# Inner Winograd sums in another order, and one subtraction and one right sum moved ahead, in a cross-attention kernel

## The chip, the cores and the metric

The kernel runs on one core of a Trainium2 chip. The metric is the device time in microseconds of one execution; three executions of the kernel before took 667.75, 667.77 and 668.99 us, a median of 667.77 us. The profile is of one further execution, which took 667.35 us, of which 665.4 us are the span from its first to its last instruction. All times of single instructions below are microseconds from the start of that span.

A core has five engines that run their own instruction streams in order and wait for one another through semaphores. Short names in the profile: PE is TensorE (matmul; PEld its weight loads), DVE is VectorE, ACT is ScalarE, POOL is GpSimd, SP is SyncE, which only issues DMAs here. GpSimd issues DMAs too, those that accumulate into on-chip memory among them.

## The reference

Eight batches of cross attention, all in fp32. `C1 = C2 = 512` channels, `N = 1024` positions, `D = 64`:

```python
q = jnp.einsum('bcn,dc->bnd', x1, Wq) + bq
k = jnp.einsum('bcn,dc->bdn', x2, Wk) + bk[:, None]
v = jnp.einsum('bcn,dc->bdn', x2, Wv) + bv[:, None]
attn = jax.nn.softmax(jnp.einsum('bnd,bdm->bnm', q, k), axis=2)
attn_out = jnp.einsum('bcm,bnm->bcn', v, attn)
return attn_out + x1
```

## The kernel before, in words

**Order of the mathematics.** The value projection is pulled behind the softmax. For each batch the kernel computes the scores transposed (`e`, two halves of 512 query positions each, 1024 keys in four tiles of 128 for each of two key groups), subtracts the column maximum (`top`), takes the exponential, then `y = x2 * e` (512 x 1024 by 1024 x 1024), scales `y` by the reciprocal of the column sums (`den`), and then `o = Wv * y`, to which `bv` and `x1` are added.

**Winograd products.** Both matrix products (stage "y" and stage "o") are split into quadrants 11, 12, 21, 22 and done with Winograd's seven products in place of eight. Left quadrants are `a` (of x2, transposed) or `w` (of Wv), right quadrants `t` (of `e`) or `y`. Sums S1 to S4 are made of the left quadrants, T1 to T4 of the right ones. The table `MULT` names the seven products by number: 1 is 11 x 11, 2 is 12 x 21, 6 is S2 x T2, 7 is S3 x T3, 5 is S1 x T1, 3 is S4 x 22, 4 is 22 x T4. Several of the seven are split once more in the same way; these have inner sums, which VectorE makes just before: `left_stream` (line 550) writes the tile `aI` of four 128x256 pieces from `LEFT` or `LEFT_SUM`, and `right_stream` (lines 573, 578, 583, 585) writes `eI`. For products 1 and 2 the four right sums are four separate instructions (line 573), since their sum is also used for the column sums (`total_0`, line 282); for the others T1 and T3 are one instruction (line 578), then T2 (583), then T4 (585). For batch n these tiles are called `aI1`, `eI2` and so on by the product; `o1`, `o7` and `o3` are products of stage "o".

**Inner products on TensorE.** `multiply_seeded` (stage "y") runs the seven inner products of one product in the order 1, 7, 6, 2, 5, 4, 3: it builds a running sum in a PSUM bank (`chain`), and ScalarE copies (line 787) seed the result's four parts from it between the steps. The step of inner product 6 goes on accumulating into `chain` only when ScalarE has copied it out. The seeds of product 1 go into bank a, those of product 2 into bank c.

**What sets the order around the change.** The schedule is written by hand: each engine's instructions run in the order in which the Python code emits them, and `weave` alternates between streams, one instruction of each in turn. `period` emits one batch `s` together with the next batch `n`: products of `y` for `s`, scores of `n`, then stage "o" of `s` while the maximum of `n` is taken off its scores (`lower`, line 340) and exponentials run on ScalarE (`exponential`, line 349), and at last the first sums of `n`. For the periods of batches 1 to 6 (`five`; `six` is batches 2 to 5), the end of the period goes like this:

- `multiply_41` interleaves product 4 of stage "y" with product 1 of stage "o". Between them `highest` folds the maximum of half 1 (line 266), and GpSimd's all-reduce (line 272) spreads it over the partitions. `complete` (line 874) closes each bank on VectorE; `evict_y` (930) and `scale_y` (916) give quadrant 21 of y, which the product of `second(2)` reads (line 485, `ps_oc<-y,w`).
- the remaining subtractions of the maximum (340) are woven with the right sums of product 7 of stage "o" (578, 583, 585, tile `eIo7`, tag `eT1`).
- `left_stream(n, 1, ...)` makes the left sums of the next batch's product 1, woven with a subtraction.
- `multiply_57` runs products 5, 7 and 3 of stage "o"; ScalarE's last seed of it is line 752. On VectorE, `complete` (line 760) waits for that seed, and `evict_o(s, "22")` (line 978, `uo`) reads quadrant 22 out; after it TensorE adds product 4 onto the same banks (`second(4)`, line 485, `ps_oc<-yT,w`).
- `early_s2` on ScalarE (`negate`, line 177) and GpSimd (an accumulating DMA, line 181) starts S2 of the next batch.
- `sum_e` (358) makes T1 of the next batch from all four tiles of `e`, `sum_t3` (384) accumulates T3 by two DMAs, then the woven right and left sums of products 1 and 2 follow, `total_0`, and `evict_o(s, "21")` (978, `o<-ps_oc`), which frees bank c.

Of the kernel before, what the change touches and what calls it, by code (L numbers as in the profile page):

```python
# [15 lines left out]
def kernel(  # L16
# [483 lines left out]
    def multiply_o1(s):  # L500
# [9 lines left out]

    LEFT = (
        ("S3", "11", "21", ALU.subtract),
        ("S1", "21", "22", ALU.add),
        ("S2", "11", "S1", ALU.subtract),
        ("S4", "12", "S2", ALU.add),
    )
    def weave(*streams):
# [13 lines left out]
    def in_turn(*streams):  # L531
# [3 lines left out]

    LEFT_SUM = (
        ("S3", "21", "11", ALU.subtract),
        ("S1", "21", "22", ALU.subtract),
        ("S2", "11", "S1", ALU.subtract),
        ("S4", "12", "S2", ALU.subtract),  # L540
    )

# [13 lines left out]
    def right_stream(s, i, x, *tags):  # L556

        half = x.shape[1] // 2
        v = {f"{q + 1}{r + 1}": x[:, ts(q, half), ts(r, H // 2)] for q in range(2) for r in range(2)}
        last = 4 // len(tags)  # L560
        shape = [P, last, half, H // 2]
        sums = [sb.tile(shape, F32, tag=t, name=f"eI{i}{t}_{s.b}") for t in tags]
        if i in (1, 2):
            for z, k in enumerate(("T1", "T2", "T4", "T3")):
                v[k] = sums[z // last][:, z % last]
            s.inner[i, "t"], s.inner[i, "m"] = v, sums[-1][:, last - 2 : last]
            for k, x, y, op in (
                ("T1", "12", "11", ALU.subtract),
                ("T3", "22", "12", ALU.add),
                ("T2", "T1", "22", ALU.add),  # L570
                ("T4", "21", "T2", ALU.subtract),
            ):
                nc.vector.tensor_tensor(v[k], v[x], v[y], op)
                yield
            return
        both, t2, t4 = sums[0][:, 0:2], sums[-1][:, last - 2], sums[-1][:, last - 1]
        part = x.rearrange("p (q k) (r n) -> p q k r n", q=2, r=2)
        nc.vector.tensor_tensor(
            both, part[:, :, :, 1, :], part[:, 0].rearrange("p k r n -> p r k n"), ALU.subtract
        )  # L580
        s.inner[i, "t"] = v | {"T1": both[:, 0], "T3": both[:, 1], "T2": t2, "T4": t4}
        yield
        nc.vector.tensor_tensor(t2, both[:, 0], v["22"], ALU.subtract)
        yield
        nc.vector.tensor_tensor(t4, v["21"], t2, ALU.add)
        yield
# [567 lines left out]
    def period(s, n, nn, nnn):  # L1154
# [54 lines left out]
        def early_s2():  # L1209
            negate(n, "S2")  # L1210
            add_11(n, "S2")
# [225 lines left out]
        if five:  # L1437
            fold(n, 1, 3, "max", ALU.max)
            products = multiply_41(s)
            next(products)  # L1440
            highest(n, 1)
            next(products, None)
            if nn:
                copy_yt4(s)
# [21 lines left out]
        if five:  # L1466
            if nn is None:
                scale_y(s, "22")
            sum_y(s, "T1")
            weave(  # L1470
                in_turn(lowers(n, 0, 2 + s.six, MH), lowers(n, 1, 0, 2)),
                right_stream(s, "o7", s.y["T3"], "eT1"),
            )
        if s.b == 0:
            add_tile(n, 0, 1)
# [32 lines left out]
        if n:  # L1508
            if five:
                sums_1 = left_stream(n, 1, n.a["11"], "i2")  # L1510
                next(sums_1)
                weave(
                    sums_1, singly(lambda: lower(n, 1, 2), *([] if nn else [lambda: sum_y(s, "T4")]))
                )
        if n is None:
            inner_right(s, "o3", s.y["22"], "eT2")
# [1 line left out]
        elif late:  # L1518
            complete_7 = multiply_57(s, while_57)
            if five:  # L1520
                if nn is None:
                    exponential(n, 1, 1)
                exponential(n, 1, 2)
                early_s2()
        else:
            complete_7 = multiply_57(s, lambda j: early_s2() if j else None)
# [10 lines left out]
            complete_7()  # L1537
        if n:
            leave = evict_o(s, "22")
        if five:  # L1540
            exponentials(n, 1, 3)
        if five:
            open_t(n)
            if nn:
# [73 lines left out]
```

## Time and profile before

| what | us |
|---|---|
| median of the runs shown (3) | 667.77 |
| profiled execution | 667.35 |
| its span | 665.4 |
| TensorE busy | 659.8 (99%) |
| VectorE busy | 626.3 (94%) |
| ScalarE busy | 379.1 (57%) |
| GpSimd busy | 208.8 (31%) |
| VectorE waiting ahead of line 760, five times | 6.2 |
| VectorE waiting ahead of line 874 of product 4, five times | 4.9 |

The granted clock is 1.0 throughout. How to read what follows: a row of the timeline gives the start, the time from the first start to the last end of the merged records, the engine, line, operation, written tile and read tiles, sizes, and how many records were merged; in brackets stands the idle time of the engine just before and what released it. Every fp32 matmul of the program is two records. Matmuls are pipelined and the ends of their records are modelled: a matmul that waits reads as busy, so stalls are found from the distances between starts. On the other engines a record's duration is some 0.08 us longer than its pitch, the distance at which the next independent instruction follows.

### The profile page before, as it was taken

The numbers are of one execution on the slowest core, as the hardware profiler recorded it, in microseconds if no ns is written. First come the engines' busy times: TensorE is split into PE (matmuls) and PEld (weight loads), VectorE is DVE, ScalarE is ACT, GpSimd is POOL, SyncE is SP. The second block draws the span as 40 slices with busy tenths as digits, with TensorE's granted clock in tenths as the row PEclk, the third lists the DMA queues.
The fourth block names the chain that finished last, engine by engine and source line by source line (L and its number), as shares of the span: only waits on it lengthen the run. The fifth ranks groups of instructions, "written<-read, shape, count | busy, mean of one in ns | idle before, by whom it ended". The sixth has DMA issues, their size and how long they took to land.

```text
span 665.4 us, 7983 instructions
## 1 busy us (share of the span) xinstructions
PE 659.8 (99%) x2626; PEld 432.7 (65%) x2626; DVE 626.3 (94%) x890; ACT 379.1 (57%) x727; POOL 208.8 (31%) x179
## 2 busy tenths in 40 slices
PE   9999999999999999999999999999999999999997
PEld 4435755766667666677666686576865757666865
DVE  1999999999999999999999999899998999999997
ACT  3755556456574575665766646756567556474332
POOL 0126215641235403263033530345213540224300
PEclk9999999999999999999999999999999999999999
DMA  9698578993889759897598895987928994376614
GB/s 334 251 287 269 107 252 154 201 284 108 276 174 216 180 155 285 180 220 197 149 280 181 197 237 162 250 175 178 272 58 189 212 211 179 74 155 160 119 40 150
DMA packets 47368, 129.05 MB, mean 194 GB/s; under 512 B 5472, under 2 KB 5984, under 8 KB 47328
## 3 DMA queue, kind: packets, MB, share of 16 engines
q0 software_dynamic: 20336, 55.12, 45.9%
q1 hardware_dynamic: 26848, 73.29, 29.7%
q8 instruction: 21, 0.34, 0.2%
q14 instruction: 19, 0.16, 0.1%
q10 hardware_dynamic: 144, 0.14, 0.1%
HBM read 87.83 MB, written 16.81 MB: 157 GB/s over the span
## 4 chain that ended last, share of the span: by engine, by line
PE 87%; DVE 11%; issue 1%; ACT 0%; DVEq 0%; ACTq 0%
PE ps_yc L596 8%; PE ps_ya L596 6%; PE ps_s L236 6%; PE ps_oa L730 6%; PE ps_oc L485 6%; PE ps_q L191 4%; PE ps_oa L485 4%; PE ps_k L191 3%; PE ps_ya L485 3%; PE ps_i7chain L596 3%; PE ps_i5chain L596 3%; PE ps_i4b L881 3%; PE ps_i3chain L596 3%; PE ps_i2chain L596 2%; PE ps_oc L881 2%; PE ps_i4chain L881 2%
## 5 line engine op out<-in xcount | busy, mean ns | idle before, releaser
L349 ACT ACTIVATE e<-e 128x1024 f32<-128x1024 f32 x60 | 63.4, 1058 | 24.4 <-DVE e L340 23.9
L340 DVE TENSOR_TENSOR e<-e,top 128x1024 f32<-128x1024 f32 x60 | 72.2, 1216 | 0.2 <-POOL top L272 0.2
L272 POOL PARTITION_ALL_REDUCE top<-max x16 | 32.0, 2000 | 104.7 <-DVE max L266 62.9
L245 ACT COPY e<-ps_s 128x512 f32<-128x512 f32 x90 | 47.7, 619 | 10.2 <-PE ps_s L236 10.1
L304 POOL PARTITION_ALL_REDUCE den<-sum x10 | 33.4, 3336 | 44.1 <-DVE sum L266 39.2
L236 PE MATMUL ps_s<-q,k 64*128 64x512 f32 (+1 forms) x188 | 46.6, 598 | 0.0
L256 DVE TENSOR_TENSOR max<-max,e 128x1024 f32<-128x1024 f32 x30 | 36.5, 1217 | 0.3
L236 PEld LDWEIGHTS ps_s<-q,k 64*128 64x128 f32 x188 | 17.5, 186 | 19.9 <-issue 17.3
L916 DVE TENSOR_TENSOR y<-y,den 128x1024 f32<-128x1024 f32 x24 | 29.2, 1219 | 0.3
L550 DVE TENSOR_TENSOR aI<-a,aI 128x256 f32<-128x256 f32 x60 | 28.1, 468 | 1.1
L787 ACT COPY ps_yc<-ps_i7chain 128x256 f32<-128x256 f32 x32 | 11.4, 357 | 30.3 <-PE ps_i7chain L596 25.6
L730 PE MATMUL ps_oa<-yT,w_S 128*128 128x512 f32 x56 | 27.5, 592 | 0.0
L285 POOL PARTITION_ALL_REDUCE den<-sum x6 | 19.4, 3228 | 25.1 <-DVE sum L266 25.1
L730 PE MATMUL ps_oa<-y,w_S 128*128 128x512 f32 x56 | 26.3, 592 | 0.0
L191 PE MATMUL ps_q<-x_in_x_dram,wqk_sb 128*64 128x512 f32 x112 | 25.6, 598 | 0.0
L787 ACT COPY ps_ya<-ps_i5chain 128x256 f32<-128x256 f32 x32 | 11.5, 360 | 24.1 <-PE ps_i5chain L596 20.0
L485 PE MATMUL ps_oa<-yT,w_S 128*128 128x512 f32 x56 | 25.2, 593 | 0.0
L485 PE MATMUL ps_oc<-yT,w 128*128 128x512 f32 x56 | 25.2, 592 | 0.0
L550 DVE TENSOR_TENSOR aI<-a 128x256 f32<-128x256 f32 x60 | 24.0, 425 | 0.0
L596 PE MATMUL ps_yc<-e,aI 128*128 128x256 f32 x92 | 23.6, 379 | 0.0
L325 POOL DMA_DIRECT2D den<-row x12 | 6.7, 560 | 53.1 <-DMA row<-few 42.3
L983 POOL DMA_DIRECT2D r<-in_x_dram x14 | 18.3, 1309 | 15.5 <-ACT r L971 15.5
(354 smaller groups left out, 1838.7 us busy)
## 6 DMA issues: line engine op xcount, KB each, us to landing
x_in_x_dram<-in_x_dram SPq DMA_DIRECT2D x60, 512.0 KB, 7.2
a<-in_x2T_dram SPq DMA_DIRECT2D x32, 512.0 KB, 5.8
aS<-in_x2T_dram POOLq DMA_DIRECT2D x21, 512.0 KB, 7.0
eT<-eT POOLq DMA_DIRECT2D x16, 512.0 KB, 11.8
r<-in_x_dram POOLq DMA_DIRECT2D x14, 512.0 KB, 7.1
uo<-in_x_dram POOLq DMA_DIRECT2D x14, 512.0 KB, 8.2
out_dram<-r SPq DMA_DIRECT2D x14, 512.0 KB, 3.3
e<-e POOLq DMA_DIRECT2D x13, 512.0 KB, 6.7
```

The source lines that it names most:

```text
L191: nc.tensor.matmul(ps[r, :], w_sb[:, c, :], s.x[:, c, ts(h, H)], start=(c == 0), stop=(c == CT - 1),)
L236: nc.tensor.matmul(ps[g][:, n], s.k[r, ts(i, P)], s.q[r, ts(h, H)][:, n], start=True, stop=True)
L245: nc.scalar.copy(e[:, g, i, :], ps[g])
L256: nc.vector.tensor_tensor(f, e[:, :, 0, :] if i == 1 else f, e[:, :, i, :], op)
L304: nc.gpsimd.partition_all_reduce(s.den[h], s.mx[h][:, 0, :], P, ReduceOp.add)
L340: nc.vector.tensor_tensor(e, e, top, ALU.subtract)
L349: nc.scalar.activation(e, e, AF.Exp)
L485: nc.tensor.matmul(ps, left[ka][:, k, ts(j, P)], right[kb][:, k, :], start=opens and k == 0, stop=i in (2, 3, 4) and k == n_k - 1, skip_gr ...
L550: nc.vector.tensor_tensor(v[k], v[x], v[y], op)
L596: nc.tensor.matmul(ps, s.inner[i][ka][:, k, :], s.inner[i, "t"][kb][:, k, :], start=opens and k == 0, stop=z in (2, 3, 4) and k == n_k - 1 ...
L730: nc.tensor.matmul(ps, w[ka][:, k, ts(j, P)], s.y[kb][:, k, :], start=False, stop=i == 3 and k == 1, skip_group_check=True,)
L881: nc.tensor.matmul(ps, s.inner[i][ka][:, k, :], s.inner[i, "t"][kb][:, k, :], start=opens and k == 0, stop=z in (2, 3, 4) and k == n_k - 1 ...
```

## The change

Three kinds of edits, all of order; no tile, shape or count of instructions changes.

1. **Inner sums.** The left sums of `LEFT` and `LEFT_SUM` go from S3, S1, S2, S4 to S3, S2, S1, S4. S2 is made from S3 and quadrant 22 instead of quadrant 11 and S1, which is the same sum. The separate right sums of products 1 and 2 go from T1, T3, T2, T4 to T3, T2, T1, T4, with T2 made from T3 and quadrant 11.
2. **Last subtraction of the maximum.** For batches 1 to 6, `lower(n, 1, 3)` and `exponential(n, 1, 3)` stood together behind `evict_o(s, "22")`. The subtraction is now woven into the left sums of the next product 1, ahead of `multiply_57`'s `complete`, and the exponential stands ahead of `early_s2`.
3. **A right sum of product 7 of stage "o".** The first instruction of `right_stream(s, "o7", ...)` (T1 and T3 at once, line 578) is emitted inside `multiply_41`, behind `highest` and ahead of the second `complete`; the rest of the stream stays where it was.

```diff
     LEFT = (
         ("S3", "11", "21", ALU.subtract),
+        ("S2", "S3", "22", ALU.subtract),
         ("S1", "21", "22", ALU.add),
-        ("S2", "11", "S1", ALU.subtract),
         ("S4", "12", "S2", ALU.add),
     )
...
     LEFT_SUM = (
         ("S3", "21", "11", ALU.subtract),
+        ("S2", "22", "S3", ALU.subtract),
         ("S1", "21", "22", ALU.subtract),
-        ("S2", "11", "S1", ALU.subtract),
         ("S4", "12", "S2", ALU.subtract),
     )
...
             for k, x, y, op in (
+                ("T3", "22", "12", ALU.add),
+                ("T2", "T3", "11", ALU.subtract),
                 ("T1", "12", "11", ALU.subtract),
-                ("T3", "22", "12", ALU.add),
-                ("T2", "T1", "22", ALU.add),
                 ("T4", "21", "T2", ALU.subtract),
             ):
...
             products = multiply_41(s)
             next(products)
             highest(n, 1)
+            sums_o7 = right_stream(s, "o7", s.y["T3"], "eT1")
+            next(sums_o7)
             next(products, None)
...
                 in_turn(lowers(n, 0, 2 + s.six, MH), lowers(n, 1, 0, 2)),
-                right_stream(s, "o7", s.y["T3"], "eT1"),
+                sums_o7,
             )
...
                 weave(
-                    sums_1, singly(lambda: lower(n, 1, 2), *([] if nn else [lambda: sum_y(s, "T4")]))
+                    sums_1,
+                    singly(lambda: lower(n, 1, 2), *([] if nn else [lambda: sum_y(s, "T4")]), lambda: lower(n, 1, 3)),
                 )
...
                 exponential(n, 1, 2)
+                exponential(n, 1, 3)
                 early_s2()
...
             leave = evict_o(s, "22")
-        if five:
-            exponentials(n, 1, 3)
         if five:
             open_t(n)
```

The order of instructions at three places on VectorE, each in the period of batch 3, whose next batch is 4 (in a tile's name the batch follows the name: `y21_3`, `aI1_4`). First the end of products 4 and o1; before:

```order
L874 TENSOR_TENSOR ps_oc1_3_1_2229<-ps_oc1_3_1_2229,v41_3_2232 128x512
L266 TENSOR_TENSOR max_4_1_2214<-max_4_1_2214 128x512
L874 TENSOR_TENSOR ps_i4b1_3_2227<-ps_i4b1_3_2227,v41_3_2232 128x512
L930 TENSOR_TENSOR y21_3_2279<-uy6_3_2027,ps_i4b1_3_2227 128x512
L930 TENSOR_TENSOR y21_3_2279<-uy6_3_2027,ps_i4b0_3_2226 128x512
L916 TENSOR_TENSOR y21_3_2279<-y21_3_2279,den_3_0_1853 128x1024
L447 TENSOR_TENSOR yT1_3_2217<-y22_3_2152,yT2_3_2218 128x1024
L340 TENSOR_TENSOR e_4_0_1987<-e_4_0_1987,top_4_0_2043 128x2x512
L578 TENSOR_TENSOR eIo7eT1_3_2286<-yT3_3_2160 128x512
```

and with the change:

```order
L874 TENSOR_TENSOR ps_oc1_3_1_2229<-ps_oc1_3_1_2229,v41_3_2232 128x512
L266 TENSOR_TENSOR max_4_1_2214<-max_4_1_2214 128x512
L578 TENSOR_TENSOR eIo7eT1_3_2265<-yT3_3_2160 128x512
L874 TENSOR_TENSOR ps_i4b1_3_2227<-ps_i4b1_3_2227,v41_3_2232 128x512
L930 TENSOR_TENSOR y21_3_2281<-uy6_3_2027,ps_i4b1_3_2227 128x512
L930 TENSOR_TENSOR y21_3_2281<-uy6_3_2027,ps_i4b0_3_2226 128x512
L916 TENSOR_TENSOR y21_3_2281<-y21_3_2281,den_3_0_1853 128x1024
L447 TENSOR_TENSOR yT1_3_2217<-y22_3_2152,yT2_3_2218 128x1024
```

Line 578 of product o7 moved up past six instructions, to stand between the fold of the maximum and the second line 874. Second the left sums of the next product 1 up to T1 of the next batch; before:

```order
L550 TENSOR_TENSOR aI1_4_2310<-a11_4_2163 128x256 x2
L340 TENSOR_TENSOR e_4_1_2165<-e_4_1_2165,top_4_1_2263 128x2x512
L550 TENSOR_TENSOR aI1_4_2310<-a11_4_2163,aI1_4_2310 128x256 x2
L573 TENSOR_TENSOR eI1yT2_4_2350<-e_4_0_1987 128x512
L760 TENSOR_TENSOR ps_oc1_3_7_2317<-ps_oc1_3_7_2317,vo7_3_2320 128x512
L978 SCALAR_TENSOR_TENSOR uo5_3_2321<-ps_oc0_3_7_2316,wqk_sb_69,uo5_3_2321 128x512
L978 SCALAR_TENSOR_TENSOR uo5_3_2321<-ps_oc1_3_7_2317,wqk_sb_69,uo5_3_2321 128x512
L340 TENSOR_TENSOR e_4_1_2165<-e_4_1_2165,top_4_1_2263 128x2x512
L358 TENSOR_TENSOR eT1_4_2358<-e_4_1_2165,e_4_0_1987 128x1024 x2
```

and with the change:

```order
L550 TENSOR_TENSOR aI1_4_2310<-a11_4_2163 128x256
L550 TENSOR_TENSOR aI1_4_2310<-a11_4_2163,aI1_4_2310 128x256
L340 TENSOR_TENSOR e_4_1_2165<-e_4_1_2165,top_4_1_2263 128x2x512
L550 TENSOR_TENSOR aI1_4_2310<-a11_4_2163 128x256
L340 TENSOR_TENSOR e_4_1_2165<-e_4_1_2165,top_4_1_2263 128x2x512
L550 TENSOR_TENSOR aI1_4_2310<-a11_4_2163,aI1_4_2310 128x256
L573 TENSOR_TENSOR eI1yT1_4_2353<-e_4_0_1987 128x512
L760 TENSOR_TENSOR ps_oc1_3_7_2318<-ps_oc1_3_7_2318,vo7_3_2321 128x512
L978 SCALAR_TENSOR_TENSOR uo5_3_2322<-ps_oc0_3_7_2317,wqk_sb_69,uo5_3_2322 128x512
L978 SCALAR_TENSOR_TENSOR uo5_3_2322<-ps_oc1_3_7_2318,wqk_sb_69,uo5_3_2322 128x512
L358 TENSOR_TENSOR eT1_4_2358<-e_4_1_2165,e_4_0_1987 128x1024 x2
```

The second line 340 moved up past the last left sum, the first right sum, line 760 and both lines 978; the left sums changed their order, and the first right sum (573) writes the buffer `yT1` instead of `yT2`. Third the sums of product 6 of batch 4; before:

```order
L550 TENSOR_TENSOR aI6_4_2431<-aS2_4_2347 128x256
L578 TENSOR_TENSOR eI6yT2_4_2433<-eT2_4_2359 128x1024
L550 TENSOR_TENSOR aI6_4_2431<-aS2_4_2347 128x256
L583 TENSOR_TENSOR eI6y21_4_2434<-eI6yT2_4_2433,eT2_4_2359 128x512
L550 TENSOR_TENSOR aI6_4_2431<-aS2_4_2347,aI6_4_2431 128x256
L585 TENSOR_TENSOR eI6y21_4_2434<-eT2_4_2359,eI6y21_4_2434 128x512
```

and with the change:

```order
L550 TENSOR_TENSOR aI6_4_2431<-aS2_4_2349 128x256
L578 TENSOR_TENSOR eI6yT2_4_2433<-eT2_4_2359 128x1024
L550 TENSOR_TENSOR aI6_4_2431<-aI6_4_2431,aS2_4_2349 128x256
L583 TENSOR_TENSOR eI6y21_4_2434<-eI6yT2_4_2433,eT2_4_2359 128x512
L550 TENSOR_TENSOR aI6_4_2431<-aS2_4_2349 128x256
L585 TENSOR_TENSOR eI6y21_4_2434<-eT2_4_2359,eI6y21_4_2434 128x512
```

The second left sum is now S2, which reads S3 of its own tile, and the third is S1. On ScalarE the exponential of the last tile (line 349) moved from behind the negation of line 177 to ahead of it. The orders of TensorE, GpSimd and SyncE are unchanged.

## The prediction, made before the changed kernel ran

> **What bounds the kernel now.** I read busy time by stretches first, then TensorE's own instructions in order of time, then what VectorE and ScalarE did at each place where TensorE's pitch breaks.
>
> ```profile
> 200.00:281.70 81.70, 81.18 (x331) 55.26 (x330) 78.32 (x113) 49.48 (x96) 27.71 (x24) 1.00 0.82 203
> 281.68:362.47 80.79, 80.79 (x330) 54.94 (x329) 77.43 (x112) 49.56 (x96) 27.66 (x24) 1.00 0.83 206
> ...
> 443.26:524.05 80.79, 80.79 (x329) 54.93 (x329) 77.45 (x112) 49.56 (x96) 27.69 (x24) 1.00 0.77 179
> ```
> The columns are the stretch, its length, then busy time on TensorE, its weight loads, VectorE, ScalarE and GpSimd, the granted clock, DMA share and GB/s. The middle periods (batches 3, 4 and 5; the first and last are shown) are equal to 10 ns, TensorE is busy in all of each, and VectorE has 3.3 us to spare. So TensorE's instruction stream sets the pace. But a stalled matmul still reads as busy here, since ends are modelled, so the starts must be read. This is TensorE around the start of batch 4:
>
> ```profile
> 364.04 1.03 PE L596 MATMUL ps_i2chain<-e,a 128*128 128x256 f32 x4
> 364.90 1.03 PE L596 MATMUL ps_i2third<-eI2eT,aI 128*128 128x256 f32 x4
> 365.89 1.13 PE L596 MATMUL ps_i2chain<-eI2eT,aI 128*128 128x256 f32 x4
> 366.86 1.03 PE L596 MATMUL ps_yc<-e,a 128*128 128x256 f32 x4
> ...
> 371.18 1.03 PE L596 MATMUL ps_i6third<-eI6yT,aI 128*128 128x256 f32 x4
> 372.17 1.10 PE L596 MATMUL ps_i6chain<-eI6y,aI 128*128 128x256 f32 x4
> 373.11 1.03 PE L596 MATMUL ps_ya<-eT,aS 128*128 128x256 f32 x4
> ```
> A group of four records has a pitch of 0.86 us (364.04 to 364.90). The third inner product of product 2 starts 0.13 late (0.99 after its forerunner), and its own group then takes 0.97, 0.11 more. Product 6 shows the same: 0.99 and 0.94. That is 0.24 and 0.21 us of stall in each period, and both are the inner product 6 of MULT, the one that reads S2 and T2. The start of batch 2 (first pair) is worse, that of batch 6 (second pair) like batch 4:
>
> ```profile
> 202.76 1.03 PE L596 MATMUL ps_i2third<-eI2eT,aI 128*128 128x256 f32 x4
> 204.31 1.13 PE L596 MATMUL ps_i2chain<-eI2eT,aI 128*128 128x256 f32 x4 [0.52 <-ACT ps_yc L787]
> ...
> 526.48 1.03 PE L596 MATMUL ps_i2third<-eI2eT,aI 128*128 128x256 f32 x4
> 527.48 1.13 PE L596 MATMUL ps_i2chain<-eI2eT,aI 128*128 128x256 f32 x4
> ```
> In batch 2 the gap is 1.55, 0.69 too long, and with 0.10 of restart 0.79 is lost; in batch 6 it is 1.00, so 0.24 with the restart. What is late:
>
> ```profile
> 364.65 1.40 DVE L978 SCALAR_TENSOR_TENSOR o<-ps_oc,wqk_sb,uo 128x512 f32<-128x512 f32 x2
> ```
> ```profile
> 365.48 0.36 ACT L787 COPY ps_yc<-ps_i2chain 128x256 f32<-128x256 f32 x1 [0.78 <-DVE o L978]
> ```
> ```profile
> 371.62 0.41 DVE L550 TENSOR_TENSOR aI<-aS,aI 128x256 f32<-128x256 f32 x1
> ```
> Product 2 of the new batch takes the bank that still holds the old batch's result quadrant 21. VectorE reads that out at 364.65, only then ScalarE seeds the bank (365.48 to 365.84), and TensorE goes on at 365.89. For product 6, the S2 sum ends at 372.03 and TensorE starts at 372.17. Both stalls are VectorE being late after the period's turn, not VectorE being short of time.
>
> **The change part by part.** It adds and removes no arithmetic: every sum, subtraction, exponential and DMA keeps its shape. Only order moves, so the prices are of waits.
>
> *The right sum of product 7, moved ahead.* VectorE waits before line 874, which closes the bank of product 4, and the moved sum fits there:
>
> ```profile
> 337.64 0.70 DVE L874 TENSOR_TENSOR ps_i4b<-ps_i4b,v 128x512 f32<-128x512 f32 x1 [0.99 <-ACT ps_i4b L890]
> ...
> 339.70 1.22 DVE L916 TENSOR_TENSOR y<-y,den 128x1024 f32<-128x1024 f32 x1
> ```
> ```profile
> 341.24 3.60 PE L485 MATMUL ps_oc<-y,w 128*128 128x512 f32 x8
> ```
> The wait of 0.99 starts at 336.65; the sum (0.6 us of pitch, 128x512, in SBUF) ends by 337.3, so line 874 starts where it did, and 0.6 us is saved later. If it did not fit, line 916, which ends at 340.92 for the products of 341.24, has 0.3 us before TensorE waits. Price between 0 and, if the whole sum were added, 0.3 a period; I take 0, since 0.6 is less than 0.99.
>
> *The last subtraction of the maximum, moved ahead.* Line 340 for the last tile of half 1 stood behind line 760, where VectorE also waits:
>
> ```profile
> 346.65 0.75 DVE L550 TENSOR_TENSOR aI<-a 128x256 f32<-128x256 f32 x2
> ...
> 348.46 0.87 DVE L550 TENSOR_TENSOR aI<-a,aI 128x256 f32<-128x256 f32 x2
> ...
> 351.28 0.70 DVE L760 TENSOR_TENSOR ps_oc<-ps_oc,vo 128x512 f32<-128x512 f32 x1 [1.35 <-ACT ps_oc L752]
> ...
> 353.51 1.22 DVE L340 TENSOR_TENSOR e<-e,top 128x1024 f32<-128x1024 f32 x1
> 354.64 2.43 DVE L358 TENSOR_TENSOR eT<-e,e 128x1024 f32<-128x1024 f32 x2
> ```
> Today the left sums end at 349.3. Less 0.6 for the sum moved above, plus 1.13 for the subtraction (its pitch, 353.51 to 354.64), they end near 349.8. Then comes the first right sum of the next product 1. It is T3 now, and in batches 3 to 5 it is written over the old T1 of y, which TensorE still reads:
>
> ```profile
> 348.97 1.02 PE L730 MATMUL ps_oa<-yT,w_S 128*128 128x512 f32 x2
> ```
> Those reads end at 349.99, so T3 runs from about 350.0 to 350.6, still ahead of the 351.28 at which line 760 is released by ScalarE. The new wait costs nothing while it ends 0.6 before the old one; without that cover it would cost what it runs over. So line 760 does not move, and all behind line 978 moves up by the 1.13 of the subtraction. Behind it line 978's read-out of quadrant 21 comes at 363.5 instead of 364.65. The bank is then free before TensorE's first inner product ends (364.90), ScalarE copies at once, and the stall of 0.24 is gone. In batch 2 the same 1.13 exceeds the 0.69. Product 6's sums come 1.13 earlier too, and its stall of 0.21 goes.
>
> *ScalarE.* The exponential that belongs to the moved subtraction goes ahead of the negation that starts S2 of the next batch:
>
> ```profile
> 352.12 1.05 ACT L177 ACTIVATE aS<-aS 128x1024 f32<-128x1024 f32 x1
> 354.76 1.06 ACT L349 ACTIVATE e<-e 128x1024 f32<-128x1024 f32 x1 [1.59 <-DVE e L340]
> ...
> 363.64 1.06 ACT L156 ACTIVATE aS<-aS 128x1024 f32<-128x1024 f32 x1
> ```
> ```profile
> aS<-in_x2T_dram POOLq DMA_DIRECT2D x21, 512.0 KB, 7.0
> ```
> The exponential runs in the 1.59 of wait, so the two sums of line 358 don't wait for it. The negation, and on GpSimd's queue the accumulating DMA of S2, come 1.0 later: issued about 354.5, landed near 361.5 by the median of 7.0. The reader is line 156 at 363.64, ScalarE's next step ahead of the seeds, so 2 us are left. On that queue the two accumulations of T3 stand behind S2's DMA; they wait for line 358, which is earlier by more than the 1.0. I take 0; bounds 0 to 0.5 a period if a DMA lands late.
>
> *Order of the inner sums.* Two unrelated 128x256 sums take 0.75, two dependent ones 0.87. Unwoven, S3, S1, S2, S4 has two dependent neighbours, S3, S2, S1, S4 one: 0.12 us of VectorE per group saved, where nothing waits for it. For product 6, S2 now stands before the T2 sum instead of behind it, 0.3 earlier: it would cure that stall alone, so it isn't counted twice. T1, T3, T2, T4 and T3, T2, T1, T4 have one dependent pair each: no difference.
>
> *Sum of the middle.* Three periods lose 0.24 + 0.21, batch 2 loses 0.79 + 0.21, batch 6 loses 0.24: 1.35 + 1.00 + 0.24 = 2.59 us, all taken as gained.
>
> **The last two batches.** From batch 6 VectorE has no wait to fill (no wait is noted at these rows), so moved work delays what it passes:
>
> ```profile
> 576.21 2.36 DVE L916 TENSOR_TENSOR y<-y,den 128x1024 f32<-128x1024 f32 x2
> ...
> 589.78 1.40 DVE L978 SCALAR_TENSOR_TENSOR uo<-ps_oc,wqk_sb,uo 128x512 f32<-128x512 f32 x2
> ```
> ```profile
> 577.72 3.60 PE L485 MATMUL ps_oc<-y,w 128*128 128x512 f32 x8
> ...
> 591.04 3.60 PE L485 MATMUL ps_oc<-yT,w 128*128 128x512 f32 x8
> ...
> 619.48 1.03 PE L596 MATMUL ps_i7chain<-e,a 128*128 128x256 f32 x4
> 620.97 1.13 PE L596 MATMUL ps_i7third<-eI7yT,aI 128*128 128x256 f32 x4 [0.47 <-DVE eI7yT L578]
> 622.00 1.10 PE L596 MATMUL ps_i7chain<-eI7yT,aI 128*128 128x256 f32 x4
> ```
> The scaling for the products of 577.72 ends at 577.4 (half of line 916's row); with 0.6 ahead of it, 578.0: TensorE loses 0.4 and 0.1 of restart. Line 978's first half ends at 590.5 for the products of 591.04; with 1.13 + 0.12 ahead it ends at 591.8, when TensorE would be at 591.5: 0.3 + 0.1 more. That is 0.9. But TensorE waits later for VectorE anyhow: 619.48 to 622.00 is 2.52 where two groups take 1.73, a stall of 0.79. VectorE's total of work up to there is the same, so the 0.9 comes out of that stall, and about 0.1 is left; the dependent pairs give back as much. I take 0 for the tail, bounds -0.3 to +0.9.
>
> Against the profiled execution's own 667.35 (span 665.4 and 1.95 around it) the sum is 667.35 - 2.59 = 664.8. The median of the runs shown is 667.77, 0.42 higher; from it the forecast is 667.77 - 2.59 = 665.2 us.
>
> **The rivals.** *The tail pays.* VectorE ends later as well, so the stall at 620.97 stays and the 0.9 comes on top: 665.2 + 0.9 = 666.1. For it: VectorE is back to back there, and any new wait adds in full. Against: the same instructions in the same stretch.
>
> *The stalls stay.* ScalarE's copy or another condition ends right behind VectorE's, or the T3 sum misses its slot: 667.8. For it: at 365.89 the wait is on ScalarE by its own line. Against: that copy notes VectorE as its releaser, with 0.78 of waiting.
>
> *The moved sum is held by GpSimd's all-reduce*, which starts in the very gap it is moved to. This one ends slower:
>
> ```profile
> 336.83 1.78 POOL L272 PARTITION_ALL_REDUCE top<-max  x1 [8.09 <-DVE max L266]
> ```
> ```profile
> 147.14 1.78 POOL L272 PARTITION_ALL_REDUCE top<-max  x1 [3.49 <-DVE max L266]
> ```
> ```profile
> 147.55 1.70 DVE L578 TENSOR_TENSOR eI3eT<-e 128x1024 f32<-128x1024 f32 x1
> ```
> At 147.55 a line 578 that started inside such an all-reduce took 1.70 and ended 0.33 after it; the first row of line 916 above gives 1.22 for that size. Held likewise, the moved sum would end at 338.9, line 874 and the scaling would come 1.25 later, and the scaling would end at 342.2 for products at 341.24: 0.9 + 0.1 lost in each of five periods. 665.2 + 5.0 = 670.2. It decides as soon as the hold passes 0.3 us. Against it: the sum starts about 336.65, 0.2 before the all-reduce. The Trainium skill (SBUF — State Buffer, Who interferes with whom) says that a VectorE instruction with two SBUF inputs and a GpSimd instruction that reads SBUF share a port, and that whichever starts first keeps it for the whole instruction. The row at 147.55 agrees; by that rule the order of two starts 0.2 us apart decides between 665.2 and 670.2.
>
> **How the numbers follow.** Forecast 0.62, tail 0.13, stalls stay 0.13, held sum 0.12. A difference of 0.2% (1.3 us) is about what a measurement here can tell from none. Faster by more than that are the forecast but for a twentieth, and most of the tail's case: 0.70; within it the stays and the rest: 0.18; slower the held sum: 0.12. The likeliest alone spans 664.4 (the tail's stall gone too, 0.79) to 666.1. The range reaches up to 667.8 to take in the tail and most of the stays, and leaves out the held sum.
>
> **What would show it.** Right: the gap before line 760 under 0.7 us; line 874's wait down by 0.6 with its start unmoved against TensorE; quadrant 21 read out 1.1 us earlier against product 2; a pitch of 0.86 through products 2 and 6; middle periods of 80.35 us; new waits of 0.3 to 0.5 in batch 6 and a smaller one before product 7 of batch 7. Wrong: a line 578 of over 1 us beside the all-reduce, a wait at line 485 in the middle periods, line 156 waiting for its DMA, or periods still 80.79.

## The result and the profile after

The changed kernel takes 665.51 us (median of 8 runs, 664.88 to 666.81), the kernel before, run beside it, 668.09 us (median of 8, 667.51 to 669.51). The ratio is 0.9961 with a 95% interval of 0.995 to 0.9972: 2.6 us less. The profiled execution of the changed kernel took 665.49 us, with a span of 663.5.

Busy time by stretches first, as before: the first and the last of the three middle periods (batches 3 and 5), from one place of a batch to the same place of the next, with the same columns.

```profile
281.35:361.70 80.35, 80.35 (x330) 55.10 (x329) 77.31 (x112) 49.56 (x96) 27.69 (x24) 1.00 0.84 206
...
442.04:522.39 80.35, 80.35 (x330) 55.11 (x329) 77.30 (x112) 49.55 (x96) 27.71 (x24) 1.00 0.77 180
```

A period is 80.35 us where it was 80.79, and VectorE's work in it is 0.12 to 0.15 less (77.31 where it was 77.43, 77.30 where it was 77.45). TensorE still reads as busy throughout, so the gain is invisible in the busy share. It stands in the starts. TensorE at product 2 and product 6 of batch 4:

```profile
363.26 1.03 PE L596 MATMUL ps_i2chain<-e,a 128*128 128x256 f32 x4
364.12 1.03 PE L596 MATMUL ps_i2third<-eI2eT,aI 128*128 128x256 f32 x4
364.99 1.03 PE L596 MATMUL ps_i2chain<-eI2eT,aI 128*128 128x256 f32 x4
365.85 1.03 PE L596 MATMUL ps_yc<-e,a 128*128 128x256 f32 x4
...
370.17 1.03 PE L596 MATMUL ps_i6third<-eI6yT,aI 128*128 128x256 f32 x4
371.03 1.03 PE L596 MATMUL ps_i6chain<-eI6y,aI 128*128 128x256 f32 x4
371.89 1.03 PE L596 MATMUL ps_ya<-eT,aS 128*128 128x256 f32 x4
```

Every group stands 0.86 or 0.87 behind its forerunner. The 0.99 and 0.97 of product 2, and the 0.99 and 0.94 of product 6, are gone. In batch 2, where 0.79 was lost, the same:

```profile
203.43 1.03 PE L596 MATMUL ps_i2third<-eI2eT,aI 128*128 128x256 f32 x4
204.30 1.03 PE L596 MATMUL ps_i2chain<-eI2eT,aI 128*128 128x256 f32 x4
```

VectorE shows why. Its rows from the end of the products 4 and o1 to the read-out of quadrant 21, in the period of batch 3, and the sum S2 of product 6 of batch 4; GpSimd's all-reduce is in the second fence, ScalarE's copy into the bank of quadrant 21 in the third:

```profile
335.80 0.69 DVE L578 TENSOR_TENSOR eIo7eT<-yT 128x512 f32<-128x512 f32 x1
336.87 0.70 DVE L874 TENSOR_TENSOR ps_i4b<-ps_i4b,v 128x512 f32<-128x512 f32 x1 [0.38 <-ACT ps_i4b L890]
...
349.33 0.69 DVE L573 TENSOR_TENSOR eI1yT<-e 128x512 f32<-128x512 f32 x1 [0.23 <-ACT e L349]
350.51 0.70 DVE L760 TENSOR_TENSOR ps_oc<-ps_oc,vo 128x512 f32<-128x512 f32 x1 [0.49 <-ACT ps_oc L752]
...
352.74 2.35 DVE L358 TENSOR_TENSOR eT<-e,e 128x1024 f32<-128x1024 f32 x2
...
362.54 1.41 DVE L978 SCALAR_TENSOR_TENSOR o<-ps_oc,wqk_sb,uo 128x512 f32<-128x512 f32 x2
...
368.57 0.41 DVE L550 TENSOR_TENSOR aI<-aI,aS 128x256 f32<-128x256 f32 x1
```
```profile
336.06 2.08 POOL L272 PARTITION_ALL_REDUCE top<-max  x1 [8.10 <-ACT ps_oa L894]
```
```profile
364.32 0.36 ACT L787 COPY ps_yc<-ps_i2chain 128x256 f32<-128x256 f32 x1 [0.40 <-PE ps_i2chain L596]
```

All of this place runs 0.77 earlier than before (line 760 at 350.51 where it was at 351.28), since the stalls of the batches ahead are gone (1.5, less the 0.7 by which this execution came to batch 1 later, see below). Against that shift the wait before line 874 falls from 0.99 to 0.38 with its start unmoved, the wait before line 760 from 1.35 to 0.49, and quadrant 21 is read out 2.11 earlier (362.54, was 364.65), which is 1.34 more than the shift: 1.13 for the subtraction, 0.12 for the order of the right sums (shown below), and 0.08 because the pair of line 358 takes 2.35 where it took 2.43. The read-out starts 0.72 ahead of product 2's first inner product; it was 0.61 behind it. ScalarE's copy, which VectorE's read-out released before, is now released by TensorE's own step. S2 of product 6 is done at 368.98, 2.05 ahead of the inner product at 371.03 that reads it; before, 0.14 ahead.

The tail pays a little. The products of batch 6 that wait for the scaling of y, and those of `second(4)` (a row at the edge of a view can hold part of its group, here the 7 of 8 records):

```profile
572.82 3.17 PE L485 MATMUL ps_oa<-yT,w_S 128*128 128x512 f32 x7
576.21 3.70 PE L485 MATMUL ps_oc<-y,w 128*128 128x512 f32 x8 [0.23 <-DVE y L916]
...
587.06 2.74 PE L730 MATMUL ps_oa<-y,w_S 128*128 128x512 f32 x6
589.95 3.27 PE L485 MATMUL ps_oc<-yT,w 128*128 128x512 f32 x7
```
```profile
618.48 1.03 PE L596 MATMUL ps_i7chain<-e,a 128*128 128x256 f32 x4
619.35 1.03 PE L596 MATMUL ps_i7third<-eI7yT,aI 128*128 128x256 f32 x4
```

At a pitch of 0.43 for two records, 576.21 is 0.39 late and 589.95 is 0.31 late. In exchange product 7 of batch 7 runs at full pitch, where 0.79 was lost. From the first inner product of one batch to that of the next, the periods are:

| from batch | before | after | difference |
|---|---|---|---|
| 1 | 81.17 | 81.18 | 0.0 |
| 2 | 81.40 | 80.35 | -1.05 |
| 3, 4, 5 (each) | 80.79 | 80.34 | -0.45 |
| 6 to TensorE's last matmul | 141.96 | 141.76 | -0.20 |

Together 2.6 us. The two spans differ by only 1.9, because the profiled execution of the changed kernel came to batch 1 0.7 later (115.34, before 114.63); this 0.7 is there 12 us after the start already, ahead of all that the change touches. In the profiled executions of all the kernels below batch 1 starts between 114.9 and 116.8, in the latest of them behind a wait for loads around 45 us, so periods are compared here, and medians for the whole.

### The profile page after: what moved, and what is told of

Same layout as the page of the kernel before. It is cut to its first block, busy times and chain, and to the rows that moved or that the text cites. A ratio compares the mean times of both kernels' runs of the same rounds, so it can differ in the third digit from the quotient of the medians.

```text
span 663.5 us, 8006 instructions
## 1 busy us (share of the span) xinstructions
PE 658.6 (99%) x2626; PEld 434.2 (65%) x2626; DVE 625.3 (94%) x890; ACT 379.0 (57%) x727; POOL 208.9 (31%) x179
## 4 chain that ended last, share of the span: by engine, by line
PE 94%; DVE 5%; issue 1%; ACT 0%
PE ps_yc L596 9%; PE ps_ya L596 7%; PE ps_oc L485 7%; PE ps_oa L730 6%; PE ps_s L236 6%; PE ps_ya L485 4%; PE ps_q L191 4%; PE ps_oa L485 4%; PE ps_i5chain L596 3%; PE ps_k L191 3%; PE ps_i7chain L596 3%; PE ps_i4b L881 3%; PE ps_i1chain L596 3%; PE ps_i2chain L596 3%; PE ps_i3chain L596 3%; PE ps_oc L881 2%
## 5 line engine op out<-in xcount | busy, mean ns | idle before, releaser
L787 ACT COPY ps_ya<-ps_i1chain 128x256 f32<-128x256 f32 x28 | 10.0, 357 | 31.6 <-PE ps_i1chain L596 28.1
```

Source lines behind the costliest of these rows:

```text
L787: nc.scalar.copy(out, of)
```

## Experiments

Each kernel was run beside the kernel before. "Period" is the distance as in the table above, in batches 3 to 5.

### Only the new order of the inner sums

```diff
+        ("S2", "S3", "22", ALU.subtract),
         ("S1", "21", "22", ALU.add),
-        ("S2", "11", "S1", ALU.subtract),
...
+                ("T2", "T3", "11", ALU.subtract),
                 ("T1", "12", "11", ALU.subtract),
```

(The whole of edit 1, with `LEFT_SUM` and T3 first.) Expected:

> Only the new order of the inner sums. Theory A (VectorE is late after the period's turn; the stalls of product 2 wait for the read-out of quadrant 21, those of product 6 for the S2 sum): the four stalls of 0.21 us before product 6 go, since S2 is made 0.3 us earlier; the stalls of product 2 (0.79 and four of 0.24) stay, since nothing ahead of the read-out gets shorter. 0.8 us less than before, ratio 0.9988. Rival B (the order is what counts, since all inner products 6 read S2 and T2): both kinds of stall go, 2.6 us less, ratio 0.9961.

Measured: 666.45 us against 668.77, ratio 0.9976 (0.9964 to 0.9988); period 80.46. The medians differ by 2.3 us, but this kernel's runs scatter from 666.1 to 668.6; by the trace 1.4 us are gained (0.22 in batch 2, three times 0.33, 0.23 from batch 6 on), nearly twice what was expected. The stall of product 6 is gone as expected, but product 2's is halved as well:

```profile
364.97 1.03 PE L596 MATMUL ps_i2third<-eI2eT,aI 128*128 128x256 f32 x4
365.85 1.13 PE L596 MATMUL ps_i2chain<-eI2eT,aI 128*128 128x256 f32 x4
366.82 1.03 PE L596 MATMUL ps_yc<-e,a 128*128 128x256 f32 x4
```

The gap is 0.88 where it was 0.99; the restart of 0.10 stays. Two later runs took the two orders apart.

### The left sums alone, the right sums alone

> Only the order of the left inner sums changes. Theory A (what the new order gained for product 2 came from the separate right sums T3, T2, T1, T4): here product 2 keeps its stall, 0.24 us in batches 3 to 6 and 0.79 in batch 2, and only product 6's stall of 0.21 goes, in batches 2 to 5: middle periods of 80.58 us, and 4 x 0.21 = 0.8 us less than before, a ratio of 0.9987. Rival (it came from the left sums, or from both together in some other way): product 2's stall shrinks here too, middle periods of about 80.46 and 1.3 to 1.6 us less, as in the run with the whole new order.

> Only the order of the separate right sums of products 1 and 2 changes. Theory A: T4 of product 2 no longer follows the T2 that it reads and starts 0.60 us after its forerunner where it started 0.72 after, so VectorE is 0.12 us earlier at quadrant 21's read-out; product 2's stall falls from 0.24 to about 0.12 in batches 3 to 6 and from 0.79 to 0.67 in batch 2. Product 6 keeps its order of sums, and its sums are up to 0.12 earlier against a TensorE that is itself 0.12 earlier: its stall stays at 0.1 to 0.21. Middle periods of 80.56 to 80.67 us, 0.5 to 0.9 us less than before, a ratio of 0.9988 to 0.9993. Rival (the order of the right sums makes no difference, as I had predicted): periods of 80.79 and a ratio of 1.000.

The left sums alone: 667.83 us against 668.45, ratio 0.9993 (0.9983 to 1.0002), period 80.58. The right sums alone: 668.00, ratio 0.999 (0.9981 to 0.9999), period 80.66. These ratios tell little from no change, but the periods, equal to 10 ns in each trace, are the two that theory A gave: 0.21 and 0.13 less than 80.79, and 0.33 together. VectorE's right sums of product 2 ahead of batch 4, first with the left sums alone reordered, then with the right sums alone:

```profile
362.64 0.68 DVE L573 TENSOR_TENSOR eI2eT<-eI2eT,e 128x512 f32<-128x512 f32 x1
363.36 0.69 DVE L573 TENSOR_TENSOR eI2eT<-e,eI2eT 128x512 f32<-128x512 f32 x1
```
```profile
362.39 0.41 DVE L550 TENSOR_TENSOR aI<-a,aI 128x256 f32<-128x256 f32 x1
362.73 0.68 DVE L573 TENSOR_TENSOR eI2eT<-eI2eT,e 128x512 f32<-128x512 f32 x1
363.33 0.68 DVE L573 TENSOR_TENSOR eI2eT<-e 128x512 f32<-128x512 f32 x1
363.93 0.68 DVE L573 TENSOR_TENSOR eI2eT<-e,eI2eT 128x512 f32<-128x512 f32 x1
```

In the old order T4 follows the T2 that it reads and starts 0.72 behind it (362.64 to 363.36). In the new order T2 reads T3, but the last left sum is woven in between, and T4 stands behind T1: both 0.60. The weave hides the dependent pair of the new order and not that of the old. The forecast of 0.67 for batch 2 missed: its period stays at 81.39. There the weave has run out of left sums one step earlier, T2 follows T3 directly and pays the 0.72 itself:

```profile
200.66 0.68 DVE L573 TENSOR_TENSOR eI2eT<-e 128x512 f32<-128x512 f32 x1
201.38 0.69 DVE L573 TENSOR_TENSOR eI2eT<-eI2eT,e 128x512 f32<-128x512 f32 x1
```

### Only the subtraction moved

```diff
-                    sums_1, singly(lambda: lower(n, 1, 2), *([] if nn else [lambda: sum_y(s, "T4")]))
+                    sums_1,
+                    singly(lambda: lower(n, 1, 2), *([] if nn else [lambda: sum_y(s, "T4")]), lambda: lower(n, 1, 3)),
...
                 exponential(n, 1, 2)
+                exponential(n, 1, 3)
                 early_s2()
...
-        if five:
-            exponentials(n, 1, 3)
```

> Only the last subtraction and its exponential moved, sums in the old order and in the old place. Theory A: the subtraction's 1.13 us fits into the 1.35 us of wait ahead of line 760 by itself, so the quadrant-21 read-out and all behind it come 1.13 us earlier; all stalls of products 2 and 6 in the middle go, 2.6 us less, ratio 0.9961; in batch 6 a new wait of 0.3 to 0.4 us before the last product 4, paid out of the stall before product 7 of batch 7. Rival C (both moves are needed, since without the 0.6 us of the right sum the subtraction runs over the wait): line 760 starts about 0.3 us late and only half is gained, 1.3 us, ratio 0.998. Rival B: 0.3 us or less.

Measured: 665.62 us, ratio 0.9957 (0.9944 to 0.997); period 80.34, and no stall at product 2 or 6 in any batch. This edit alone gives all that the change gives. Its wait in batch 6, before `second(4)`, was larger than expected, 0.65 us:

```profile
587.82 2.31 PE L730 MATMUL ps_oa<-y,w_S 128*128 128x512 f32 x5
590.62 1.55 PE L485 MATMUL ps_oc<-yT,w 128*128 128x512 f32 x3 [0.49 <-DVE uo L978]
```

With the whole change it is 0.31. The o7 sum is then ahead of the scaling instead, where it costs 0.39 more. So VectorE's lateness in batch 6 is paid at one place or at two.

### Only the right sum of product o7 moved

```diff
             highest(n, 1)
+            sums_o7 = right_stream(s, "o7", s.y["T3"], "eT1")
+            next(sums_o7)
             next(products, None)
```

> Only the right sum of product o7 moved. Theory A: the 0.6 us saved ahead of line 760 are lost again in the wait for ScalarE there (1.35 becomes 1.95 us), so nothing behind it moves: 0.0 us, ratio 1.000; in batch 6 a new wait of about 0.4 us before the product that reads quadrant 21 of y, paid out of the later stall. Rival C: 0.6 us earlier all the way, the stalls of 0.24 and 0.21 go and 0.79 shrinks to about 0.2, 2.0 us less, ratio 0.997.

Measured: 668.56 us, ratio 0.9998 (0.9989 to 1.0007); period 80.79, the stalls of products 2 and 6 as before, and the expected wait in batch 6 (0.37 before `ps_oc<-y,w`). No gain, as expected. VectorE's two waits say where the 0.6 went:

```profile
338.52 0.70 DVE L874 TENSOR_TENSOR ps_i4b<-ps_i4b,v 128x512 f32<-128x512 f32 x1 [0.39 <-ACT ps_i4b L890]
...
352.16 0.70 DVE L760 TENSOR_TENSOR ps_oc<-ps_oc,vo 128x512 f32<-128x512 f32 x1 [1.95 <-ACT ps_oc L752]
```

The wait before line 874 is 0.60 shorter and the one before line 760 is 0.60 longer (1.95, was 1.35). Both are released by ScalarE, and ScalarE by TensorE, so work moved out from between them only makes the second wait longer.

### The same sum, started inside the all-reduce

```diff
             highest(n, 1)
             sums_o7 = right_stream(s, "o7", s.y["T3"], "eT1")
-            next(sums_o7)
             next(products, None)
+            next(sums_o7)
```

This is the changed kernel with the sum one step later, behind the second line 874, so that it begins after GpSimd. It was made to price the rival in which the all-reduce holds the sum.

> The change, but the right sum of o7 is emitted behind the second line 874, so that it starts while GpSimd's all-reduce of the maximum runs (it starts 0.2 us behind the fold and takes 1.8 us). If the all-reduce holds such an instruction to its end (the slower rival of the prediction): line 578 takes over 1.0 us instead of 0.69 in batches 1 to 5, in batch 6 about 2 us; line 916 ends 0.9 us later and TensorE loses 0.6 to 0.7 us in each of five periods and over 1 us in batch 6: 3 to 4 us more than the change. If it isn't held: 0.69 us, TensorE loses about 0.35 us a period, 1.7 to 2.0 us more than the change.

Measured: 667.56 us, ratio 0.9985 (0.9976 to 0.9993); period 80.66, a stall of 0.21 and a restart of 0.1 before `ps_oc<-y,w`, and 0.80 there in batch 6. By the trace it is 2.1 us slower than the change (0.45 in batch 1, 0.31 in each of the next four, 0.41 from batch 6 on). In the middle periods the sum was not held, in batch 6 it was (VectorE, then GpSimd, of batch 3; then the same two of batch 6):

```profile
337.81 0.68 DVE L578 TENSOR_TENSOR eIo7eT<-yT 128x512 f32<-128x512 f32 x1
```
```profile
336.39 1.78 POOL L272 PARTITION_ALL_REDUCE top<-max  x1 [8.10 <-DVE max L266]
```
```profile
574.14 1.23 DVE L578 TENSOR_TENSOR eIo7eT<-yT 128x512 f32<-128x512 f32 x1
```
```profile
573.80 1.77 POOL L272 PARTITION_ALL_REDUCE top<-max  x1 [23.42 <-PE ps_i4b L881]
```

At 337.81 the all-reduce has 0.36 of its recorded time left, and the sum takes its normal 0.68. At 574.14 it has 1.43 left, and the sum takes 1.23, 0.55 more, and still ends (575.37) before the all-reduce does (575.57). So the all-reduce does hold such a sum, but not to its recorded end (the last section says for how long), and an unheld sum at that place costs 0.31 a period by itself: line 916 starts 2.51 behind the second line 874, where it is 2.06 with the change, and TensorE waits for it.

### Quadrant 21 read out earlier, by another way

```diff
             if five:
+                evict_o(s, "21")
                 total_0(n)
             else:
                 total(n, 0)
-            evict_o(s, "21")
+                evict_o(s, "21")
```

The kernel before with the read-out put ahead of the column sums. If the lateness of this read-out were the whole cause, product 2 would gain as with the change.

> The kernel before, but for batches 1 to 6 the read-out of quadrant 21 is emitted ahead of the column sums of half 0 instead of behind them; none of the change's edits. Theory A: the read-out comes 1.9 us earlier (lines 282 and 266), the stalls of product 2 go (0.79 + four of 0.24 = 1.75 us), those of product 6 stay, since the work ahead of them is the same: 1.75 us less, ratio 0.9974. If the stalls of product 2 wait for something else (ScalarE's queue, or the negation of S2), nothing changes: ratio 1.000.

Measured: 675.46 us, ratio 1.0104 (1.0089 to 1.0118); period 81.98. Product 2's stalls are gone, as expected, but product 6, which was expected to keep its 0.21, now loses 1.06 and 0.40 and the restarts, and the whole is 7 us slower: a miss. What was not expected stands ahead of product 6 of batch 4, on VectorE, GpSimd and TensorE:

```profile
370.92 4.04 DVE L358 TENSOR_TENSOR eT<-eT,e 128x1024 f32<-128x1024 f32 x2
```
```profile
370.51 3.23 POOL L285 PARTITION_ALL_REDUCE den<-sum  x1 [5.64 <-DVE sum L266]
```
```profile
376.48 1.13 PE L596 MATMUL ps_i6third<-eI6yT,aI 128*128 128x256 f32 x4 [0.90 <-DVE eI6yT L578]
377.84 1.10 PE L596 MATMUL ps_i6chain<-eI6y,aI 128*128 128x256 f32 x4 [0.23 <-DVE aI L550]
```

The same two sums in the kernel before:

```profile
366.57 2.71 DVE L358 TENSOR_TENSOR eT<-eT,e 128x1024 f32<-128x1024 f32 x2
```

The all-reduce over the column sums starts 0.41 ahead of the two sums of line 358 and holds them: 4.04 us, where the kernel before has 2.71 and an undisturbed pair 2.35 (352.74 above). In the old order the all-reduce starts at 364.84, right behind the read-out of quadrant 21 at 364.65, which takes 1.40 beside it as it does elsewhere, and these sums come 1.73 behind its start. The read-out was the cover for the all-reduce, so the step that looked late could not simply be moved up.

### The last two batches

Three variants of the changed kernel. The first puts both moved steps of batch 6 back to their old places:

```diff
-            next(sums_o7)
+            if nn:
+                next(sums_o7)
...
-                    singly(lambda: lower(n, 1, 2), *([] if nn else [lambda: sum_y(s, "T4")]), lambda: lower(n, 1, 3)),
+                    singly(lambda: lower(n, 1, 2), (lambda: lower(n, 1, 3)) if nn else (lambda: sum_y(s, "T4"))),
...
-                exponential(n, 1, 3)
+                if nn:
+                    exponential(n, 1, 3)
...
+        if five and nn is None:
+            exponentials(n, 1, 3)
```

> The change, but batch 6 keeps both moved steps at their old places (the order of the inner sums stays new). Theory: the two new waits of TensorE in batch 6 (0.39 + 0.1 and 0.31 + 0.1 us) go, and TensorE then waits for VectorE before product 7 of batch 7 as it did before (0.7 to 0.8 us): no gain over the change, within 0.2 us. Rival (the tail pays for them): 0.9 us less than the change, ratio to before 0.995.

Measured: 665.15 us, ratio 0.9949 (0.9937 to 0.9962); the stretch from batch 6 to the end 141.62, with the change 141.76. Both waits of batch 6 are gone and the stall before product 7 of batch 7 is back, 0.52 at this start and more behind it:

```profile
617.88 1.03 PE L596 MATMUL ps_i7chain<-e,a 128*128 128x256 f32 x4
619.26 1.13 PE L596 MATMUL ps_i7third<-eI7yT,aI 128*128 128x256 f32 x4 [0.36 <-DVE eI7yT L578]
```

The same time is lost at another place. The second and third variant also make the left sums of product 4 of batch 7 later, to free VectorE ahead of product 7, one on the change and one on the variant above:

```diff
                 add_t4(s)
-                inner_left(s, 4, s.a["22"], "a12")
...
             else:
+                inner_left(s, 4, s.a["22"], "a12")
                 inner_right(s, 3, s.t["22"], "eT1")
```

> The change, but in batch 7 the left sums of product 4 (1.5 us of VectorE) are made behind product 5 instead of ahead of its end, so the sums of product 7 come 1.5 us earlier. Theory: the changed kernel has no stall left there (its new waits in batch 6 have used it up), so nothing is gained: within 0.2 us of the change. Rival: VectorE's lateness still costs there, up to 0.8 us less.

> Both: batch 6 keeps the old places, and the left sums of product 4 of batch 7 come later. Theory: neither alone gains, together they do, since the waits of batch 6 go and the stall before product 7 of batch 7 has no cause: 0.8 to 0.9 us less than the change, ratio to before about 0.995, time about 664.7 where before is 668.1. If another VectorE wait takes over behind it (the sums of product 4 and quadrant 12 are back to back up to the last product), 0.3 us or less.

Measured: 666.76 us, ratio 0.9968 (0.9955 to 0.9981), stretch 142.08; and 665.85 us, ratio 0.9961 (0.9949 to 0.9973), stretch 142.40. The first gains nothing, as expected, but its stretch is 0.3 longer than with the change, where 0.2 was allowed. The second is a miss: 0.8 to 0.9 was expected to come free, and the stretch is 0.8 longer than without the move. Product 7 runs free, and TensorE waits further on (TensorE, then VectorE, of the second):

```profile
632.70 0.70 PE L881 MATMUL ps_oa<-eIo1i,w_I 128*128 128x256 f32 x2 [0.76 <-DVE y L932]
```
```profile
621.46 0.18 DVE L318 RECIPROCAL few<-few 128x4 f32<-128x4 f32 x1 [1.10 <-DMA few<-den]
```

Without the move VectorE works back to back from product 7 of batch 7 to the sums of product o1, no wait of its own among them: the tail there is bound by the amount of VectorE's work. With the move VectorE reaches the reciprocals of line 318 before the DMA that brings their input has landed, and stands idle for 1.10 us (0.80 in the first of the two). The expectation had not named that wait. No variant is told from the change by its interval; the first has the lowest ratio, and the intervals overlap.

## Why the prediction was right, and where it was not

**The sum.** Forecast -2.59, measured -2.6 by the medians and by the table of periods. Term by term: three periods of 0.45 each, measured 0.45; batch 2 1.00, measured 1.05; batch 6 and the tail 0.24, measured 0.20.

**The subtraction.** Right, and shown by itself: alone it takes both stalls out of every period. The step that carried it was that line 760, against TensorE, does not start earlier when VectorE has less to do and does not start later when VectorE has 1.13 more, as long as that fits into the 1.35 of wait. T3 over the old T1 came as worked out: TensorE's last reads were forecast to end at 349.99, which with the 0.77 of shift is 349.22, and T3 starts at 349.33. The profile's row names ScalarE's exponential there, but T3 reads only the `e` of half 0, whose last exponential started at 342.96 and took 1.05; the reads of the old T1 are what had just ended:

```profile
348.20 1.02 PE L730 MATMUL ps_oa<-yT,w_S 128*128 128x512 f32 x2
```

**The right sum of o7.** The price of 0 was right. "0.6 us is saved later" was not: alone, the sum's 0.6 goes into the wait before line 760 (1.35 to 1.95) and the time is the same. With the subtraction moved too it leaves more cover ahead of line 760, but the subtraction fits without it: alone, it left 0.3 of the wait there. In batch 6 the sum costs the forecast 0.4 at line 916. So no gain of the change is shown to come from this edit.

**The held sum.** The rival fell with the change itself: line 578 took 0.69, as an undisturbed one does, and the all-reduce that started 0.26 behind it took 2.08 where it took 1.78. The Trainium skill (SBUF — State Buffer, Who interferes with whom) gives the shared port to whichever of the two starts first; this trace agrees, the all-reduce is the one that waited, and nothing waits for it there. The rival's point of decision was about right: with line 916 0.45 later TensorE stalled by 0.21. Its price was not borne out: the forecast took the 0.33 by which the row at 147.55 ended behind its all-reduce for a sum of half that size, and the one held sum of the experiment ended 0.20 ahead of it; in the middle periods the sum that began inside the all-reduce wasn't held at all. Both held rows have start plus extra time at 0.89 us after the all-reduce's start (0.41 + 0.48, 0.34 + 0.55). By that a held sum in the change would have ended at 338.4 (336.83 + 0.89 + 0.68), an estimate, and not at 338.9.

**The order of the inner sums.** This term was put at nothing and was mis-sized. "T1, T3, T2, T4 and T3, T2, T1, T4 have one dependent pair each: no difference" counted pairs in the list and not in the order that `weave` emits. For product 2 of batches 3 to 6 the new order has none left, 0.12 us is saved directly ahead of the late read-out, and product 2's stall is halved by that alone. It did not change the forecast, since the subtraction clears the same stall with 1 us to spare. That S2 ahead of T2 cures product 6's stall alone was right (period 80.58).

So edits 1 and 2 remove the same stalls and their gains don't add: by the traces 1.4 us and 2.5 us alone, 2.6 with all three edits.

**ScalarE and the DMAs.** The price of 0 was right: line 156, which reads the accumulated S2, starts with no wait noted, and the two sums of line 358 follow at once behind line 978 (352.74 above):

```profile
362.87 1.06 ACT L156 ACTIVATE aS<-aS 128x1024 f32<-128x1024 f32 x1
```

**The tail.** The waits of 0.4 and 0.3 in batch 6 came as forecast (0.39 and 0.31), and were paid out of the stall before product 7 of batch 7. The "smaller one" that should have stayed there did not. That the new order of the sums gave back the rest fits the run with this order alone, in which that stall is 0.50 at its first start where it was 0.63 before. The rival in which the tail pays fell; putting the two steps back in batch 6 moves the loss and changes the stretch by 0.14.

## What to carry to other kernels

Find stalls of a pipelined engine in the distances between starts, and ask for each what the late engine was waiting for earlier in the same period: work taken from behind that wait and put ahead of it is free up to the wait's length, and all that follows comes earlier by it. Work that only moves from one wait's approach to another's buys nothing. Before a late step is moved itself, see what it covers. Where streams are woven, count dependent neighbours in the emitted order.

## What the runs showed of the hardware

**An all-reduce holds VectorE's sums from SBUF for part of its recorded time.** Three starts of the same 128x512 sum against the same 1.78 us all-reduce: 0.26 ahead, 0.69; 0.34 behind, 1.23; 1.42 behind, 0.68. Instructions that read PSUM (line 978, 1.40 beside the all-reduce of line 285) kept their time. The Trainium skill's section (SBUF — State Buffer, Who interferes with whom) says that the one that starts first keeps the port for the whole instruction; here it is free before the recorded end. How long before can be worked out: a held sum's start plus its extra time is the same point whatever its size and start. It is 0.89 us after the start of the 1.78 us all-reduce (the two held rows worked out above), and for the 3.23 us all-reduce of line 285 it is 2.09 in the kernel before (1.73 + 0.36) and 2.10 with the early read-out (0.41 + 1.69). If a held sum waits first and then runs at its own speed, the sums from SBUF are let go 0.89 us ahead of the recorded end of the one and 1.13 ahead of that of the other, an estimate. It fits the sum that began 0.36 ahead of the end and was not held. The Trainium skill (Perfetto Trace Analysis, GPSIMD Engine Instruction) calls a GpSimd instruction's span in a profile unreliable, which would fit: the recorded end need not be when the port comes free.

**A dependent neighbour on VectorE costs 0.12 us.** 0.72 instead of 0.60 for 128x512, in the pairs above. The Trainium skill (VectorE: DVE Perf Modes, The DRAIN you can't avoid) reports that a chain of copies takes the same with a semaphore after each as with one at the end, and does not say whether each waits for the one before. Here the sums that wait on the forerunner's semaphore start 0.12 later than those that do not, and with the right sums alone it was worth 0.13 us a period.

**A pause of TensorE of 1.5 us was followed by half the clock.** In the variant with the early read-out TensorE waited before product 6 of batch 2, and the granted clock of the stretch behind it (the column after the five engines' busy times) was 0.52 for 3.4 us, with a pitch of 1.71 for a group in place of 0.86:

```profile
212.19:215.61 3.42, 3.42 (x9) 2.67 (x9) 3.38 (x6) 1.50 (x3) 0.67 (x1) 0.52 1.11 207
```
```profile
210.82 1.13 PE L596 MATMUL ps_i6third<-eI6yT,aI 128*128 128x256 f32 x4 [1.45 <-DVE eI6yT L578]
212.19 1.92 PE L596 MATMUL ps_i6chain<-eI6y,aI 128*128 128x256 f32 x4 [0.23 <-DVE aI L550]
213.90 1.91 PE L596 MATMUL ps_ya<-eT,aS 128*128 128x256 f32 x4
```

In the later batches of the same variant the pause was 0.90 and the clock stayed at 1.0. So a stall of 1.5 us there cost 1.7 more. This was seen once; how long a pause has to be for it, no run shows. The Trainium skill (TensorE: Matmul & The Clock Gate, What's actually happening) gives an idle window of about 3.4 us for the fall to half; this one was shorter.
